# A two-layer relational graph convolution: edge tiles grouped by eight, one wait, one placing product and one addition per group

## The chip, the cores and the metric

The kernel runs on one core of one Trainium2 chip. The metric is the device time of one execution in microseconds (us); the number quoted is the median of three executions. A separate execution was recorded by the hardware profiler; it has its own time, which is given beside its span below.

## What is computed

The graph has N = 12,500 nodes with C = 128 float32 features and E = 200,000 edges, sorted by destination. The type of an edge (10 relations) is the argmax over ten of the 42 columns of its attributes. Two layers of the following form, a relu between them, and a layer norm over the sum with the input:

```python
seg  = dst * NUM_REL + edge_type
sums = segment_sum(x[src], seg, N * NUM_REL)
cnt  = segment_sum(ones, seg, N * NUM_REL)
mean = (sums / maximum(cnt, 1)[:, None]).reshape(N, NUM_REL, -1)
layer(x) = einsum('nrd,rdo->no', mean, w_rel) + x @ root + bias
...
h = relu(layer1(x))
out = layernorm(x + layer2(h))
```

So each layer reads 200,000 rows of 512 bytes by index, sums them by (destination, relation), divides by the count, multiplies each relation's means by that relation's 128x128 matrix and adds over relations.

## The kernel before

**Tiles.** The edges are cut into 1563 tiles of 128 (`NT`). Since they are sorted, the destinations of a tile lie in a window of at most 12 nodes (`WN`) from its first; a flag is set on the chip where that or another assumption fails, and a general program at the end of the file then does the work over (it is not run with these inputs).

**Per tile, in a layer** (`edges`). `gather` lets GpSimd (POOL) issue an indirect DMA that brings the 128 source rows to SBUF (L352). VectorE (DVE) makes a 128x120 matrix `oh` (L366): in an edge's row, the column 12 x type + (destination - window start) holds the edge's weight, one over its count; all else is 0. TensorE (PE) multiplies the gathered rows with it (L368): `zp` holds, for each feature, the mean's contributions to 120 (relation, node) pairs. In the profile a float32 matmul appears as two passes. ScalarE (ACT) copies four tiles at a time to `zs` (L369). For every 16 tiles ten products, one per relation with its 128x128 matrix as the stationary operand and 16x12 = 192 moving columns, accumulate `po` in PSUM (L373). Then, for each tile, DVE adds 12 columns of `po` to `acc`, a 128 x 12,628 array of features by nodes that stays in SBUF (L381); where, comes from a register loaded from the list of window starts `bt` (L376). The groups at the end have 8 and 3 tiles.

**Blocks.** When all edges of a block of 512 nodes are surely past (a fixed slack of 10 tiles), it is finished (25 blocks, the last of 212 nodes): the block's own rows are loaded and transposed (L297, copied by ACT in L299), the root product and the transposed sums are accumulated (L302, L303). In layer 1 (`hidden`) relu and the store to `hD` follow (L317), in layer 2 (`final`) the residual, the statistics, the normalisation and the store of the output (L332 to L342). `acc` is cleared behind each block.

**Preparation.** For each chunk of 128 tiles (13 chunks): `sources` loads source indices, casts them (L121), transposes them on PE (L113) and leaves the index list `idxE` (L114); `types` finds the relations (L180 to L185), keys and flags; `count` compares each edge's key with its 40 neighbours on either side, one shift at a time (L259, 40 compares and 80 products with the identity, L260 and L261, which add them up), and leaves the weights `wE`. Chunk 0 (and the sources and types of chunk 1) are prepared ahead of layer 1; the others in steps between the tiles of layer 1, by `between`, which takes as many steps as bring the chunk to its end eight tiles before it is needed.

**Order.** The instructions of each engine stand in the order of the program as scheduled; every tile buffer comes from a pool, and a new use waits for the last reader of the old one. `gpool` holds 22 buffers of four tiles, so POOL may run 88 tiles ahead of PE. `dpool` holds 12 one-hot matrices, `ps_z` three PSUM buffers of four tiles, `ps_o` a single one for `po`. Loads and stores of blocks and of preparation go through the queue of SyncE (SP). POOL waits for nothing but its index list, the buffers of the ring and, in layer 2, the store of `hD`. At the start DVE clears the whole of `acc` with one instruction (L155).

Of the kernel before, what the change touches and what calls it, by code (L numbers as in the profile page):

```python
# [9 lines left out]
F32 = mybir.dt.float32  # L10
BF16 = mybir.dt.bfloat16
I32 = mybir.dt.int32
# [14 lines left out]
Q = 4  # L27
G = 16
RING = 22
# [3 lines left out]
SLACK = 10  # L33
# [7 lines left out]
def rgcn_resnorm_kernel(ctx: ExitStack, tc: tile.TileContext, x, src, dst, attr, w_rel1, root1, b1,  # L41
# [12 lines left out]

    nc = tc.nc
# [5 lines left out]
    NCH = -(-NT // CT)  # L61
    NPAD = N + W
    NBLK = -(-N // YB)
# [15 lines left out]
    prep = fast.enter_context(tc.tile_pool(name="prep", bufs=2))  # L79
    msgp = fast.enter_context(tc.tile_pool(name="msgp", bufs=2))  # L80
    eqp = fast.enter_context(tc.tile_pool(name="eqp", bufs=6))
    gpool = fast.enter_context(tc.tile_pool(name="gpool", bufs=RING))
    dpool = fast.enter_context(tc.tile_pool(name="dpool", bufs=12))
    zpool = fast.enter_context(tc.tile_pool(name="zpool", bufs=2))
    ps_z = fast.enter_context(tc.tile_pool(name="ps_z", bufs=3, space=PSUM))
    ps_o = fast.enter_context(tc.tile_pool(name="ps_o", bufs=1, space=PSUM))
    ps_k = fast.enter_context(tc.tile_pool(name="ps_k", bufs=1, space=PSUM))
    ps_c = fast.enter_context(tc.tile_pool(name="ps_c", bufs=1, space=PSUM))
# [20 lines left out]
    def to_edges(to, t, c):  # L109

        p = chunk_rows(c)
        pt = ps_c.tile([P, P], F32, name="pt")
        nc.tensor.transpose(pt[:, :p], t[:p], ident[:p, :p])  # L113
        nc.vector.tensor_copy(to[:, c * CT:c * CT + p], pt[:, :p])  # L114
# [14 lines left out]

    thr_i = const.tile([P, NCH], I32, name="thr_i")  # L130
    nc.gpsimd.iota(thr_i, pattern=[[CT, NCH]], base=-SLACK, channel_multiplier=1)
    pads = const.tile([P, L + 1], I32, name="pads")
    nc.gpsimd.iota(pads, pattern=[[1, L + 1]], base=FAR, channel_multiplier=0)
    lane = const.tile([P, P], F32, name="lane")
# [8 lines left out]
    thr = const.tile([P, NCH], F32, name="thr")  # L143
    nc.vector.tensor_scalar(thr_i, thr_i, 6, None, op0=ALU.arith_shift_right)
    nc.vector.tensor_scalar(thr, thr_i, float(YB), None, op0=ALU.mult)
# [5 lines left out]
    nc.vector.tensor_tensor(own, own, lane, op=ALU.add)  # L151
    fl = const.tile([P, 1], F32, name="fl")
    nc.vector.memset(fl, 0.0)
    acc = const.tile([P, NPAD], F32, name="acc")
    nc.vector.memset(acc, 0.0)  # L155
# [5 lines left out]
    bt = keep.tile([1, NT], I32, name="bt")  # L161
# [25 lines left out]
    def types(c):  # L187
# [13 lines left out]
        nc.sync.dma_start(bt[:, c * CT:c * CT + n], bass.AP(dst.tensor, b, [[1, 1], [P, n]]))  # L201
        if last:
            nc.sync.dma_start(bt[:, NT - 1:NT], bass.AP(dst.tensor, dst.offset + E - P, [[1, 1], [1, 1]]))
# [392 lines left out]
```

## Time and profile before

| | |
|---|---|
| median of 3 runs | 4014.53 us (4013.73 to 4018.22) |
| the profiled execution's own time | 4817.36 us |
| its span, first to last instruction | 4815.5 us |
| mean granted TensorE clock in it | 0.706 |
| POOL busy, of it in gathers | 2971.9 us, 2970.6 us |
| PE busy | 2439.3 us |
| DVE busy | 1585.0 us |
| ACT busy | 470.9 us |
| longest single wait of POOL (for `hD`, between the layers) | 74.2 us |

The profiled execution is 803 us longer than the median of the others. The page gives, for each engine, the time in which it executed instructions; for groups of instructions (line, engine, output<-input, shape, count) the busy time, the mean length of one in ns, and the idle time of the engine just before them with what ended most of it. "issue" there is idle time that ended without anything waited for. In the waits, the three figures are the total in us, how often, and the longest. In the timeline, each row has its start in us, its length, engine, line and operation, and in brackets the idle time ahead of it and what ended it.

### The profile page before, as it was taken

To read this page: it belongs to the slowest core of one execution; us is meant where nothing else is said; L and a number is where in the kernel's file an instruction comes from. 1 tells how busy PE (TensorE), PEld (TensorE's weight loads), DVE (VectorE), ACT (ScalarE), POOL (GpSimd) and SP (SyncE) were. 2 spreads that over 40 slices of the span, in tenths; PEclk is the share of its full clock that TensorE was granted. 3 is DMA by queue.
4 is the path that set the end of the run, shared out by engine and by line. 5 is a ranking of instruction groups with operands and counts; after the bars stand their busy time and mean duration, and the time that the engine had idled before them with its cause. 6 is when DMAs were issued, how large, how long until landed. Compare 5 with 4: busy or idle time off the path is not lost.

```text
span 4815.5 us, 44360 instructions
## 1 busy us (share of the span) xinstructions
PE 2439.3 (51%) x12272; PEld 2184.5 (45%) x12272; DVE 1585.0 (33%) x7623; ACT 470.9 (10%) x899; POOL 2971.9 (62%) x3136
## 2 busy tenths in 40 slices
PE   0456655655655565665615444444444444444456
PEld 0445554545555455555514443444444444444445
DVE  3333443344334333333302222232222322232234
ACT  0001110111011111111100100000000000000001
POOL 6566666666666666666266666666666666666661
PEclk9766676676767676666756677777777776776777
DMA  5121222122122221112111221112111211121110
GB/s 163 41 75 51 79 76 75 53 76 75 51 80 74 56 55 52 50 51 54 32 48 46 55 53 49 49 52 55 50 51 51 57 51 50 50 56 49 51 52 25
DMA packets 180408, 279.04 MB, mean 58 GB/s; under 512 B 55448, under 2 KB 127015, under 8 KB 177031
## 3 DMA queue, kind: packets, MB, share of 16 engines
q0 software_dynamic: 100032, 205.07, 16.2%
q1 hardware_dynamic: 76957, 69.59, 4.6%
q8 instruction: 108, 1.77, 0.2%
q10 hardware_dynamic: 3168, 1.44, 0.1%
q14 instruction: 143, 1.17, 0.1%
HBM read 262.28 MB, written 13.60 MB: 57 GB/s over the span
## 4 chain that ended last, share of the span: by engine, by line
PE 29%; issue 27%; another core or an unknown queue 24%; DVE 8%; POOL 7%; ACT 2%; DMA 1%; DVEq 1%; SPq 0%; ACTq 0%; POOLq 0%
PE zp L368 14%; PE po L373 12%; POOL g L352 7%; DVE oh L366 4%; DVE acc L381 3%; ACT zs L369 1%; PE pf L303 1%; PE pt L261 1%; PE pt L260 1%; PE pf L302 1%; DMA g<-in_x_dram,idxE 1%; DVEq L376 1%; ACT fT L299 0%; PE pf L297 0%
## 5 line engine op out<-in xcount | busy, mean ns | idle before, releaser
L352 POOL DMA_INDIRECT g<-hD,idxE x1563 | 1477.4, 945 | 946.9 <-issue 429.4
L368 PE MATMUL zp<-oh,g 128*128 128x120 f32 x6252 | 1269.8, 364 | 1551.8 <-issue 1001.8
L352 POOL DMA_INDIRECT g<-in_x_dram,idxE x1563 | 1493.2, 955 | 802.9 <-issue 416.1
L368 PEld LDWEIGHTS zp<-oh,g 128*128 128x128 f32 x6252 | 1134.9, 267 | 1675.4 <-issue 1105.0
L366 DVE TENSOR_SCALAR oh<-iota,keyE,wE 128x120 f32<-128x120 f32 x3126 | 1028.5, 351 | 675.4 <-remote 340.8
L381 DVE TENSOR_TENSOR acc<-acc,po 128x12 f32 x3126 | 518.1, 166 | 2032.6 <-remote 1268.1
L373 PE MATMUL po<-zs,w 128*128 128x192 f32 x3960 | 916.7, 386 | 439.6 <-issue 225.3
L373 PEld LDWEIGHTS po<-zs,w 128*128 128x128 f32 x3960 | 807.2, 232 | 507.5 <-issue 301.7
L369 ACT ACTIVATE zs<-zp 128x480 f32<-128x480 f32 (+1 forms) x782 | 417.8, 570 | 3650.1 <-remote 2408.5
L259 DVE TENSOR_TENSOR eqb<-kp,kh 128x129 bf16<-128x129 f32 (+43 forms) x520 | 148.4, 305 | 196.5 <-remote 145.3
L260 PE MATMUL pt<-eqb,identb 128*128 128x128 bf16 (+1 forms) x520 | 120.9, 269 | 160.0 <-issue 130.7
L261 PE MATMUL pt<-eqb,identb 128*128 128x128 bf16 (+1 forms) x520 | 121.6, 275 | 52.6 <-issue 49.7
L261 PEld LDWEIGHTS <-identb 128*128 128x128 bf16 (+1 forms) x520 | 62.8, 121 | 176.2 <-issue 170.3
L302 PE MATMUL pf<-root,fT 128*128 128x128 f32 x392 | 105.3, 359 | 55.9 <-issue 41.0
L303 PE MATMUL pf<-ident,a 128*128 128x128 f32 x392 | 107.4, 365 | 13.9 <-issue 8.1
L302 PEld LDWEIGHTS pf<-root,fT 128*128 128x128 f32 x392 | 84.3, 263 | 63.9 <-issue 48.0
L260 PEld LDWEIGHTS <-identb 128*128 128x128 bf16 (+1 forms) x520 | 66.8, 129 | 75.4 <-issue 74.9
L303 PEld LDWEIGHTS pf<-ident,a 128*128 128x128 f32 x392 | 88.2, 270 | 22.5 <-issue 14.5
L299 ACT ACTIVATE fT<-pf 128x512 f32<-128x512 f32 (+1 forms) x50 | 29.3, 587 | 498.7 <-remote 245.3
L332 DVE TENSOR_TENSOR v<-pf,xb 128x512 f32<-128x512 f32 (+2 forms) x26 | 17.1, 660 | 174.7 <-remote 127.3
L297 PE MATMUL pf<-ident,hb 128*128 128x128 f32 x98 | 21.9, 356 | 23.9 <-DVE v L332 17.6
L342 DVE TENSOR_SCALAR o<-v,mv,rstd 128x128 f32<-128x128 f32 x98 | 27.8, 349 | 0.2
(71 smaller groups left out, 371.6 us busy)
## 6 DMA issues: line engine op xcount, KB each, us to landing
m<-in_edge_attr_dram SPq DMA_DIRECT2D x24, 1344.0 KB
g<-in_x_dram,idxE POOLq DMA_INDIRECT x1563
g<-hD,idxE POOLq DMA_INDIRECT x1563
xb<-in_x_dram SPq DMA_DIRECT2D x48, 256.0 KB
hD<-hb SPq DMA_DIRECT2D x24, 256.0 KB
hb<-hD SPq DMA_DIRECT2D x24, 256.0 KB
out_dram<-o SPq DMA_DIRECT2D x24, 256.0 KB
w<-in_L_gnn_w_rel_dram ACTq DMA_DIRECT2D x2, 640.0 KB
```

Of the source, the lines that this page charges most:

```text
L259: nc.vector.tensor_tensor(eq[:p, :P + d], kp[:p, L - d:L + P], kh[:p, L:L + P + d], op=ALU.is_equal)
L260: nc.tensor.matmul(pc[:p], identb[:p, :p], eq[:p, :P], start=(d == 1), stop=False)
L261: nc.tensor.matmul(pc[:p], identb[:p, :p], eq[:p, d:d + P], start=False, stop=(d == L))
L302: nc.tensor.matmul(pr[:h, t, :], fT[:, t * P:t * P + h], rsb[l], start=True, stop=False)
L303: nc.tensor.matmul(pr[:h, t, :], a[:, t * P:t * P + h], ident, start=False, stop=True)
L352: nc.gpsimd.indirect_dma_start(out=g[:, j, :], out_offset=None, in_=table, in_offset=bass.IndirectOffsetOnAxis(ap=idxE[:, t0 + j:t0 + j + ...
L366: nc.vector.tensor_scalar(oh, iota[:, :KW], keyE[:, t:t + 1], wE[:, t:t + 1], op0=ALU.is_equal, op1=ALU.mult)
L368: nc.tensor.matmul(zp[:, j, :], g[:, j, :], oh, start=True, stop=True)
L369: nc.scalar.activation(zs[:, :, q:q + m, :], zp[:, :m].rearrange("c j (r n) -> c r j n", n=WN), AF.Copy)
L373: nc.tensor.matmul(po[:, :n], wsb[l][:, r, :], zs[:, r, :n], start=(r == 0), stop=(r == NREL - 1))
L376: _, offs = nc.values_load_multi_w_load_instructions(bt[0:1, t0 + j0:t0 + j0 + m], engines=[DVE], min_val=0, max_val=N - 1, skip_runtime_b ...
L381: nc.vector.tensor_tensor(acc[:, s], acc[:, s], po[:, j0 + j], op=ALU.add)
```

## The change

- A group is 8 tiles, in both layers. One-hot matrices, gathered rows and `zp` have one buffer per group; the ring is 13 groups, 104 tiles. Of the eight zp products of a group the last tile's is issued first, and it alone waits, for all eight gathers.
- The projection takes the sums as the stationary operand (up to 96 columns, node slots of 8 tiles) and the relation's matrix as 128 moving columns. Its result has node slots on partitions; ACT copies it to SBUF (`ms`). A second product multiplies it with a 96x80 matrix `at` of zeros and ones that DVE makes for each group; it places the slots of all 8 tiles in a window of 80 nodes (`pa`), with features on partitions again. One DVE addition of 128x80 per group takes it into `acc`; four groups' positions are loaded into registers at a time.
- The stages of three groups are interleaved: sums of one, then placing and addition of an older, then projection of the one between.
- `types` makes the slots' positions (`place`) with a small product per chunk and a check of their width; 25 loads of single destinations serve a check that a block was not finished too early. The time at which a block is finished comes from a formula (`done_after`); blocks are 24 of 512 nodes, then 128 and 84.
- `count` compares 8 shifts in one instruction (5 instead of 40) and adds them with 20 products of 512 columns instead of 80 of 128; a reduction adds the four parts.
- The preparation's pools have one buffer instead of two.
- `acc` is cleared at the start in pieces of 512 columns, written ahead of `sources(1)`; it isn't cleared behind the blocks of layer 2. The flag's reduction stands between the layers instead of behind the second.

The constants for the slots' positions, the small loads into `b8_i` and the lines in which only names of PSUM tiles change are left out of the diff below.

```diff
-Q = 4
-G = 16
-RING = 22
+G = 8
+QB = 4
+SW = 80
+RING = 13
+DB = 8
 L = 40
 CT = 128
 YB = 512
-SLACK = 10
...
-    NBLK = -(-N // YB)
+    starts = list(range(0, N - YB // 2, YB))
+    starts += list(range(starts[-1] + YB, N, P)) if N - starts[-1] > YB else []
+    NBLK = len(starts)
+    def done_after(k):
+        if k == NBLK - 1:
+            return NT
+        f = starts[k + 1] / N
+        return min(NT, int((E * f + 5 * (E * f * (1 - f)) ** 0.5) / P) + 2)
...
-    prep = fast.enter_context(tc.tile_pool(name="prep", bufs=2))
-    msgp = fast.enter_context(tc.tile_pool(name="msgp", bufs=2))
-    eqp = fast.enter_context(tc.tile_pool(name="eqp", bufs=6))
+    prep = fast.enter_context(tc.tile_pool(name="prep", bufs=1))
+    eqp = fast.enter_context(tc.tile_pool(name="eqp", bufs=2))
     gpool = fast.enter_context(tc.tile_pool(name="gpool", bufs=RING))
-    dpool = fast.enter_context(tc.tile_pool(name="dpool", bufs=12))
-    zpool = fast.enter_context(tc.tile_pool(name="zpool", bufs=2))
-    ps_z = fast.enter_context(tc.tile_pool(name="ps_z", bufs=3, space=PSUM))
+    dpool = fast.enter_context(tc.tile_pool(name="dpool", bufs=3))
+    zpool = fast.enter_context(tc.tile_pool(name="zpool", bufs=3))
+    spool = fast.enter_context(tc.tile_pool(name="spool", bufs=3))
+    ps_z = fast.enter_context(tc.tile_pool(name="ps_z", bufs=2, space=PSUM))
     ps_o = fast.enter_context(tc.tile_pool(name="ps_o", bufs=1, space=PSUM))
-    ps_k = fast.enter_context(tc.tile_pool(name="ps_k", bufs=1, space=PSUM))
-    ps_c = fast.enter_context(tc.tile_pool(name="ps_c", bufs=1, space=PSUM))
+    ps_a = fast.enter_context(tc.tile_pool(name="ps_a", bufs=1, space=PSUM))
...
     acc = const.tile([P, NPAD], F32, name="acc")
-    nc.vector.memset(acc, 0.0)
...
-    bt = keep.tile([1, NT], I32, name="bt")
+    bt = keep.tile([1, NG], I32, name="bt")
+    place = keep.tile([GR, NCH * CT // G], F32, name="place")
+    wide = const.tile([P, 1], F32, name="wide")
+    nc.vector.memset(wide, 0.0)
+    late_i = const.tile([1, NBLK], I32, name="late_i")
 
...
-        nc.sync.dma_start(bt[:, c * CT:c * CT + n], bass.AP(dst.tensor, b, [[1, 1], [P, n]]))
-        if last:
-            nc.sync.dma_start(bt[:, NT - 1:NT], bass.AP(dst.tensor, dst.offset + E - P, [[1, 1], [1, 1]]))
+        ng = -(-p // G)
+        nc.sync.dma_start(bt[:, c * CT // G:c * CT // G + ng], bass.AP(dst.tensor, b, [[1, 1], [G * P, ng]]))
+        b8_i = prep.tile([G, CT // G], I32, name="b8_i")
...
+        for k in range(NBLK):
+            t = done_after(k)
+            if c * CT <= t < c * CT + p:
+                nc.sync.dma_start(late_i[:, k:k + 1], bass.AP(dst.tensor, dst.offset + t * P, [[1, 1], [1, 1]]))
...
-        nc.vector.tensor_scalar(bt[:, c * CT:c * CT + p], bt[:, c * CT:c * CT + p], 0, N - 1, op0=ALU.max,
-                                op1=ALU.min)
+        g0 = c * CT // G
+        nc.vector.tensor_scalar(bt[:, g0:g0 + ng], bt[:, g0:g0 + ng], 0, N - 1, op0=ALU.max, op1=ALU.min)
+        b8 = prep.tile([G, CT // G], F32, name="b8")
+        nc.vector.tensor_copy(b8[:, :ng], b8_i[:, :ng])
+        pw = ps_f.tile([P, YB], F32, name="pf")
+        nc.tensor.matmul(pw[:GR, :ng], rank, b8[:, :ng], start=True, stop=True)
+        nc.vector.tensor_scalar(place[:, g0:g0 + ng], pw[:GR, :ng], within, None, op0=ALU.add)
+        reach = prep.tile([GR, 1], F32, name="reach")
+        nc.vector.tensor_reduce(reach, place[:, g0:g0 + ng], axis=AX.X, op=ALU.max)
+        nc.vector.tensor_tensor(wide[:GR], wide[:GR], reach, op=ALU.max)
...
-        kp = ps_k.tile([P, P + 2 * L], F32, name="kp")
-        nc.scalar.activation(kp[:p], kh[:p], AF.Copy)
-        pc = ps_c.tile([P, P], F32, name="pt")
-        for d in range(1, L + 1):
-            eq = eqp.tile([P, P + L], BF16, name="eqb")
-            nc.vector.tensor_tensor(eq[:p, :P + d], kp[:p, L - d:L + P], kh[:p, L:L + P + d], op=ALU.is_equal)
-            nc.tensor.matmul(pc[:p], identb[:p, :p], eq[:p, :P], start=(d == 1), stop=False)
-            nc.tensor.matmul(pc[:p], identb[:p, :p], eq[:p, d:d + P], start=False, stop=(d == L))
-            if d % 2 == 0:
-                yield
+        kp = ps_f.tile([P, YB], F32, name="pf")
+        nc.scalar.activation(kp[:p, :P + 2 * L], kh[:p], AF.Copy)
+        pc = ps_f.tile([P, 4, P], F32, name="pf")
+        R = P + L
+        for d in range(1, L + 1, DB):
+            eq = eqp.tile([P, DB, R], BF16, name="eqb")
+            ahead = bass.AP(kh.tensor, kh.offset + d, [[kh.ap[0][0], p], [1, DB], [1, R]])
+            nc.vector.tensor_tensor(eq[:p], kp[:p, None, :R].to_broadcast([p, DB, R]), ahead, op=ALU.is_equal)
+            for k in range(0, DB, 4):
+                nc.tensor.matmul(pc[:p], identb[:p, :p], eq[:p, k:k + 4, L:], start=(d + k == 1), stop=False)
+                back = bass.AP(eq.tensor, eq.offset + k * R + L - d - k, [[eq.ap[0][0], p], [R - 1, 4], [1, P]])
+                nc.tensor.matmul(pc[:p], identb[:p, :p], back, start=False, stop=(d + k + 3 == L))
+            yield
         wp = prep.tile([P, P], F32, name="wp")
-        nc.vector.tensor_scalar(wp[:p], pc[:p], 1.0, None, op0=ALU.add)
+        nc.vector.tensor_reduce(wp[:p], pc[:p].rearrange("p k e -> p e k"), axis=AX.X, op=ALU.add)
+        nc.vector.tensor_scalar(wp[:p], wp[:p], 1.0, None, op0=ALU.add)
...
-        nc.vector.memset(acc[:, n0:n0 + n], 0.0)
+        if l == 0:
+            nc.vector.memset(acc[:, n0:n0 + n], 0.0)
...
-        g = gpool.tile([P, Q, C], F32, name="g")
+        g = gpool.tile([P, G, C], F32, name="g")
+        return g, [nc.gpsimd.indirect_dma_start(out=g[:, j, :], out_offset=None, in_=table, in_offset=(
+            bass.IndirectOffsetOnAxis(ap=idxE[:, t0 + j:t0 + j + 1], axis=0))) for j in range(n)]
+    whole = mybir.DependencyInfo(mybir.DependencyClass.Sync, mybir.DependencyReason.DATA)
+    def sums(table, t0, n):
+        g, gathers = gather(table, t0, n)
+        oh = dpool.tile([P, G, KW], F32, name="oh")
         for j in range(n):
...
+            t = t0 + j
+            nc.vector.tensor_scalar(oh[:, j, :], iota[:, :KW], keyE[:, t:t + 1], wE[:, t:t + 1], op0=ALU.is_equal,
+                                    op1=ALU.mult)
+        at = spool.tile([GR, SW], F32, name="at")
+        nc.vector.tensor_scalar(at, iota[:GR, :SW], place[:, t0 // G:t0 // G + 1], None, op0=ALU.is_equal)
+        zp = ps_z.tile([P, G // QB, YB], F32, name="zp")
+        for j in reversed(range(n)):
+            m = nc.tensor.matmul(zp[:, j // QB, j % QB * KW:(j % QB + 1) * KW], g[:, j, :], oh[:, j, :],
+                                 start=True, stop=True)
+            if j < n - 1:
+                tc.keep_in_program_order(m)
+                continue
+            for d in gathers[:j]:
+                tc.add_manual_dep(m.ins, d.ins.name, whole, reason="one wait per group")
+        return zp, at
+    def project(l, n, zp):
 
         zs = zpool.tile([P, NREL, G, WN], F32, name="zs")
...
+        for b in range(-(-n // QB)):
+            m = min(QB, n - b * QB)
+            nc.scalar.activation(zs[:, :, b * QB:b * QB + m, :],
+                                 zp[:, b, :m * KW].rearrange("c (j r n) -> c r j n", r=NREL, n=WN), AF.Copy)
+        po = ps_o.tile([P, C], F32, name="po")
         for r in range(NREL):
-            nc.tensor.matmul(po[:, :n], wsb[l][:, r, :], zs[:, r, :n], start=(r == 0), stop=(r == NREL - 1))
...
+            nc.tensor.matmul(po[:n * WN], zs[:, r, :n].rearrange("c j n -> c (j n)"), wsb[l][:, r, :],
+                             start=(r == 0), stop=(r == NREL - 1))
+        ms = spool.tile([GR, C], F32, name="ms")
+        nc.scalar.activation(ms[:n * WN], po[:n * WN], AF.Copy)
+        return ms
+    offs = []
+    def add(t0, n, ms, at):
+        pa = ps_a.tile([P, SW], F32, name="pa")
+        nc.tensor.matmul(pa, ms[:n * WN], at[:n * WN], start=True, stop=True)
+        if not offs:
+            g0 = t0 // G
+            offs.extend(nc.values_load_multi_w_load_instructions(
+                bt[0:1, g0:min(NG, g0 + 4)], engines=[DVE], min_val=0, max_val=N - 1,
+                skip_runtime_bounds_check_because=HELD)[1])
+        s = ds(offs.pop(0), SW)
+        nc.vector.tensor_tensor(acc[:, s], acc[:, s], pa, op=ALU.add)
 
     def layer(table, l, finish, steps):
 
         done = 0
...
+        held, projected = [], []
+        def project_oldest():
+            t0, n, zp, at = held.pop(0)
+            projected.append((t0, n, project(l, n, zp), at))
+        def add_oldest():
+            nonlocal done
+            t0, n, ms, at = projected.pop(0)
+            add(t0, n, ms, at)
+            while done < NBLK and t0 + n >= done_after(done):
                 finish(done)
                 done += 1
+        for t0 in range(0, NT, G):
+            n = min(G, NT - t0)
+            held.append((t0, n, *sums(table, t0, n)))
+            if projected:
+                add_oldest()
+            if len(held) > 1:
+                project_oldest()
+            if steps:
+                till, left, s = steps[0]
+                for _ in range(max(1, -(-left[0] // max(1, till - t0 // G)))):
+                    left[0] -= 1
+                    if next(s, steps) is steps:
+                        steps.pop(0)
+                        break
+        while held or projected:
+            if projected:
+                add_oldest()
+            if held:
+                project_oldest()
 
...
+    for a in range(0, NPAD, YB):
+        nc.vector.memset(acc[:, a:min(NPAD, a + YB)], 0.0)
     sources(1)
     for _ in chain(types(0), types(1)):
...
-        todo.append((c * CT - 8, [8 + L // 2 + 2], chain(*s, count(c))))
+        todo.append((c * CT // G - 2, [8 + L // DB + 2], chain(*s, count(c))))
     layer(x, 0, hidden, todo)
-    layer(hD, 1, final, [])
+    late = const.tile([1, NBLK], F32, name="late")
+    for k in range(NBLK):
+        if done_after(k) < NT:
+            nc.vector.tensor_scalar(late[:, k:k + 1], late_i[:, k:k + 1], float(starts[k + 1]) - 0.5, None, op0=ALU.is_lt)
+        else:
+            nc.vector.memset(late[:, k:k + 1], 0.0)
+    nc.vector.tensor_scalar(wide, wide, float(SW) - 0.5, None, op0=ALU.is_gt)
+    nc.vector.tensor_tensor(fl, fl, wide, op=ALU.max)
     pf = ps_f.tile([P, YB], F32, name="pf")
     nc.tensor.transpose(pf[0:1, :P], fl, ident)
-    flag_f = const.tile([1, 1], F32, name="flag_f")
-    nc.vector.tensor_reduce(flag_f, pf[0:1, :P], axis=AX.X, op=ALU.max)
-    nc.vector.tensor_copy(flag_i, flag_f)
+    flag_f = const.tile([1, 2], F32, name="flag_f")
+    nc.vector.tensor_reduce(flag_f[:, 0:1], pf[0:1, :P], axis=AX.X, op=ALU.max)
+    nc.vector.tensor_reduce(flag_f[:, 1:2], late, axis=AX.X, op=ALU.max)
+    nc.vector.tensor_tensor(flag_i, flag_f[:, 0:1], flag_f[:, 1:2], op=ALU.max)
+    layer(hD, 1, final, [])
     fast.close()
```

## The prediction

> **What bounds the kernel now.** I read the page's table of busy shares first, then the groups and the waits, and last the timeline of single stretches. The median to explain is 4014.53 us. The profiled execution took 4817.36 us, span 4815.5 and 1.9 outside it, so it is 803 us longer than the median; a prediction needs to know which part of it is in the plain runs too.
>
> ```profile
> PE 2439.3 (51%) x12272; PEld 2184.5 (45%) x12272; DVE 1585.0 (33%) x7623; ACT 470.9 (10%) x899; POOL 2971.9 (62%) x3136
> ...
> L352 POOL DMA_INDIRECT g<-hD,idxE x1563 | 1477.4, 945 | 946.9 <-issue 429.4
> L352 POOL DMA_INDIRECT g<-in_x_dram,idxE x1563 | 1493.2, 955 | 802.9 <-issue 416.1
> ```
>
> No engine is full; POOL is busiest, all of it in gathers (L352), one per tile and layer. Its waits, and its timeline at the end of a layer:
>
> ```profile
> POOL g L352 <- issue: 845.5, 2763, 1.8
> POOL g L352 <- PE zp L368: 479.2, 124, 6.1
> POOL g L352 <- remote: 196.4, 101, 14.7
> ```
>
> ```profile
> 2297.02 0.94 POOL L352 DMA_INDIRECT g<-in_x_dram,idxE  x1 [0.30 <-issue]
> 2372.20 0.94 POOL L352 DMA_INDIRECT g<-hD,idxE  x1 [74.24 <-DMA hD<-hb]
> ```
>
> "Issue" is 845.5/2763 = 0.306 us ahead of nearly every gather, waiting for nothing. A gather of 0.94 us and its gap repeat every 1.2487 us ((3182.16-3163.43)/15, in a stretch without waits). That is the number everything rests on: 1563 gathers make 1562 x 1.2487 = 1950.5 us a layer. Layer 1's total is 1493.2-1563x0.944 = 17 us more, layer 2's 1.6. Now the plain run as this stream plus its ends: first gather at 15.39; 1967.5; from the last gather of layer 1 to layer 2's first 31.1 (2.74 until PE may read it, as from 2372.20 to the first zp at 2374.94, and 28.4 from the last three tiles' zp at 2343.83 to 2372.20); 1952.1; tail 2.74 and 46.2 (last zp's end, about 4769.3, to 4815.5); 1.9 outside. Sum 4016.9, within 0.1% of the median. So the plain runs have no room for POOL's waits for the ring (479.2, 196.4 and smaller ones): they, and a layer gap of 74 instead of 30, are the profiled execution's 803 us. The kernel is a gather stream with three ends.
>
> Whether PE keeps pace is read where POOL is silent. The rows of the two stretches after a layer's last gather:
>
> ```profile
> 4724.51 3.83 PE L368 MATMUL zp<-oh,g 128*128 128x120 f32 x32 [1.81 <-ACT zs L369]
> 4729.63 3.52 PE L373 MATMUL po<-zs,w 128*128 128x192 f32 x20 [1.29 <-DVE acc L381]
> 4733.86 3.83 PE L368 MATMUL zp<-oh,g 128*128 128x120 f32 x32 [0.72 <-ACT zs L369]
> ```
>
> Sixteen tiles pass in 9.35 us (4724.51 to 4733.86), 0.58 us each against 1.25 of the gather. Beside gathers the same trace has PE taking a pass in 2 to 3 us with "issue" ahead of it (2429 to 2456 us): stalls that end with the gathers, and that the sum has no place for.
>
> **What the Trainium skill says.** "DMA: Bandwidth & Descriptors", section on the anatomy of a gpsimd-issued DMA, gives about 2.0 us of fixed cost, mostly completion: the trace has 2.74 from the gather's start to PE, of which 0.94 is POOL's; they pipeline, so the 1.25 stands. "Perfetto Trace Analysis", on such instructions, says that GpSimd's processors write the descriptors in place of a hardware block: 0.94 us for every gather, whichever table it reads, agrees. "SBUF — State Buffer", on who interferes, says that a DVE instruction with two SBUF inputs contends with a GpSimd one that reads SBUF: gathers of 1.2 to 1.5 us in layer 1 lie beside argmax's L182 and L183, which fits the 17 us. "TensorE: Matmul & The Clock Gate", on what is happening, says that PE runs at half clock after idling: passes here take 0.12 us (3.83/32) or 0.21 to 0.22 (the tail's 36-column po: 4.45/20), so I cost PE at both.
>
> **The change, part by part.**
>
> *Gathers.* 3126 as before, one a tile, same rows. Removed 0, added 0: the stream stays 1967.5 + 1952.1. POOL's few more iotas at the start are of 0.1 to 0.3 us each, before its first gather and beside DVE's clearing; nothing.
>
> *PE's load.* Per 8 tiles: 16 zp passes, 20 po passes (ten float32 products, now for 8 tiles instead of 16), 2 placing passes: 38, against 26. At 0.12 us 4.6 us, at 0.22 8.4 us, in the 9.99 us that 8 gathers take (8x1.2487). Finish adds 12 matmuls (24 passes) every 64 tiles, layer 1 the counts besides (20 matmuls of 512 columns instead of 80 of 128, every 128 tiles). Hidden under the gathers while a pass stays below about (9.99-0.9)/38 = 0.239 us; above that it is the rival below.
>
> *One wait per 8 tiles.* The first zp pass waits for the last of eight gathers; the other fifteen, the po of the group before and everything behind them on PE wait with it. This delays PE by up to seven gathers, 8.7 us, but nobody waits for it except the ring, which grows from 88 to 104 tiles (110 to 130 us of gathers). Cost 0, at the two layer ends counted below.
>
> *Additions and register loads.* 3126 additions of 0.166 us, with register loads between them, become 392 of 128x80, each between 0.166 (128x12) and 0.35 (L342, 128x128). No gain: DVE, at 33% of the span, is hidden under the gathers, and the one-hots (3126, 1028.5 us) stay. ACT gets one copy of 128 columns more a group, under the 0.57 of its 480-column copy (L369), in 9.99: hidden.
>
> *Counting by 8 shifts, single prep buffers.* 40 compares of 0.305 become 5 of 128x1344; hidden while the 104-tile ring holds. SP has about 61 transfers ahead of the first keys' load in place of 24; SP's rows for such small loads are 0.4 to 0.9 us each, so at 0.6 the first counts start 22 us later than the 49 us of the trace. The ring is full only at 9.7+104x1.2487 = 139 us, which leaves some 68 for the counts. Cost 0; if that cover went, each us late is a us.
>
> *Clearing in pieces.* Before:
>
> ```profile
> 3.52 10.58 DVE L155 MEMSET acc<- 128x12628 f32 x1 [2.60 <-issue]
> 14.02 0.16 DVE L121 CAST s_f<-s_i 128x128 f32<-128x128 int32 x1
> ...
> 15.39 1.11 POOL L352 DMA_INDIRECT g<-in_x_dram,idxE  x1 [13.50 <-DVE own L151]
> ```
>
> The first index list (L121) stands behind the whole clear. In the changed program's order on DVE, 4 pieces stand ahead of that cast and 8 more between it and the index copy. The 13 pieces of 512 columns, at 10.58x512/12628 = 0.43 us: 12 make 5.2, so 3.5+5.2+1.4 (cast to gather, 15.39-14.02) = 10.1; if the source rows' arrival rules, 8.5. I take 9.7: gain 5.7, bounds 3 to 9.
>
> *Between the layers.* Before, behind the last zp: one po of 16 tiles (3.48), an addition chain of 4.43, po of 8 and 3 with the last waits, root, relu, store: 28.4 us. After: the last group of 3 needs zp, copy, po (20 passes), copy, placing (2), addition, then a block of only 84 nodes instead of 212. In the changed order, PE has behind the last zp two po (40 passes), three placing products (6) and the last three blocks' finish (36 passes at most). Estimate: 82 passes are 10 us at 0.12 or 18 at 0.22; the copies, additions, relu and the store between them come to 7 to 10.5. So 17 to 28.5; I take 23: gain 5.4, bounds 0 to 12.
>
> *Tail.* Before, behind the last zp:
>
> ```profile
> 4771.03 3.52 PE L373 MATMUL po<-zs,w 128*128 128x192 f32 x20 [0.87 <-DVE acc L381]
> 4778.99 6.51 PE L373 MATMUL po<-zs,w 128*128 128x192 f32 x20 [4.43 <-DVE acc L381]
> ...
> 4799.78 4.45 PE L373 MATMUL po<-zs,w 128*128 128x36 f32 x20 [2.73 <-DVE acc L381]
> ```
>
> po has one buffer, so each next one waits for 16 separate additions (4.43). That goes; the flag's matmul and reductions move between the layers' programs, where they stand beside the first gathers. What comes late next is the layernorm of the last blocks: 84 rows' worth of v, statistics, o and a store, some 10 us as before. With the sum above plus this, 22 to 33.5; I take 29: gain 17, bounds 5 to 24 (and not below 0, since every removed wait was on the path).
>
> *Sum.* 9.7 + 1967.5 + 2.74+23 + 1952.1 + 2.74+29 + 1.9 = 3988.7, 28 less than the same sum before; taken from the median, 4014.5-28 = 3986.5. Predicted 3987.
>
> **Rivals.**
>
> *A, the forecast:* the stream binds, the ends get shorter. Its own range from the bounds: gains of 8 to 44, 3971 to 4006. For it: the closing sum. Chance 0.66.
>
> *B, the ends give nothing:* three stages of 8 tiles at slow passes, with the last group's extra copy and placing, make gap and tail as long as before, and only the start's few us remain: 4007 to 4022, within 0.2% (8 us, about what this measurement can tell from no change). For it: PE idles between groups, so slow passes at the end are likely. Chance 0.13.
>
> *C, slower: PE becomes the bound.* Place: po, now twice as often, 38 passes a group. If PE idles while it waits for eight gathers and starts each burst slow, passes cost 0.22 and more with gaps at each change of tile; it decides from 0.239 us a pass. At 0.26: 38x0.26+0.9 = 10.8 against 9.99, 8% on 3920: about 4320. For it: 0.22 is common in the trace, and layer 1 has finish and counts as well. Against: a PE that is busy throughout has fast passes. Chance 0.12.
>
> *D, the stalls of the profiled execution are real:* the plain interval would be shorter than 1.25 (the median less stalls), and fewer instructions and waits would take several per cent: 3600 to 3950. Against: it needs an interval that no row shows. Chance 0.09.
>
> **How the numbers follow.** Faster: A nearly whole, and D: 0.75. Same: B: 0.13. Slower: C: 0.12. The range 3965 to 4014 is A's bounds, a little beyond on the short side for the estimated passes, and half of B; what lies outside is C, D and the rest of B.
>
> **What would show it.** Gathers still 1.2487 us apart with 0.94 each; first gather near 10 us; the stretch from layer 1's last gather to layer 2's first near 26; last gather to the end near 32; PE and DVE idle ahead of each group on gathers. POOL waiting on zp for whole stretches while PE has no gap speaks for C. An interval below 1.2 us would show the premise wrong, and the sum with it.

## The result, and the profile after

| | before | changed |
|---|---|---|
| median | 4014.43 us (20 runs, 4012.07 to 4020.32) | 4021.74 us (20 runs, 4016.72 to 4028.73) |
| ratio | 1 | 1.0018, 95% interval 1.0012 to 1.0025 |

So the change costs 7 us where 28 were to be gained. The changed kernel's profiled execution took 4026.78 us, close to its median, and its trace has none of the long stalls in which the one before stood. The waits of POOL and its groups on the page, changed kernel:

```profile
POOL g L404 <- issue: 929.2, 3049, 0.3
POOL g L404 <- DMA hD<-hb: 19.5, 1, 19.5
```

```profile
L404 POOL DMA_INDIRECT g<-in_x_dram,idxE x1563 | 1521.9, 974 | 482.4 <-issue 464.5
L404 POOL DMA_INDIRECT g<-hD,idxE x1563 | 1498.9, 959 | 495.5 <-issue 464.7
```

Inside a layer POOL stands only in the fixed 0.3 us ahead of each gather: the stream of gathers does set the pace. But a gather takes 974 and 959 ns on the mean, not the 955 and 945 of before. The ends of the two layers in POOL's timeline:

```profile
9.28 1.29 POOL L404 DMA_INDIRECT g<-in_x_dram,idxE  x1 [6.33 <-DVE lane L172]
...
2006.27 0.94 POOL L404 DMA_INDIRECT g<-in_x_dram,idxE  x1 [0.30 <-issue]
2026.74 0.94 POOL L404 DMA_INDIRECT g<-hD,idxE  x1 [19.53 <-DMA hD<-hb]
...
4000.67 0.94 POOL L404 DMA_INDIRECT g<-hD,idxE  x1 [0.30 <-issue]
```

The kernel before is compared through a run of it whose only edit is the clearing in pieces (e4 below), since that profiled execution is undisturbed too (span 4009.5). Its same four gathers:

```profile
8.71 1.51 POOL L351 DMA_INDIRECT g<-in_x_dram,idxE  x1 [6.83 <-DVE lane L150]
...
1976.54 0.95 POOL L351 DMA_INDIRECT g<-in_x_dram,idxE  x1 [0.30 <-issue]
2008.21 0.94 POOL L351 DMA_INDIRECT g<-hD,idxE  x1 [30.72 <-DMA hD<-hb]
...
3962.50 0.94 POOL L351 DMA_INDIRECT g<-hD,idxE  x1 [0.30 <-issue]
```

Subtracting starts gives the whole account (start of before: 15.39 of its own trace):

| us | before | changed | difference | predicted |
|---|---|---|---|---|
| first gather | 15.4 | 9.3 | -6.1 | -5.7 |
| stream, layer 1 | 1967.8 | 1997.0 | +29.2 | 0 |
| between the layers | 31.7 | 20.5 | -11.2 | -5.4 |
| stream, layer 2 | 1954.3 | 1973.9 | +19.6 | 0 |
| last gather to the end | 47.0 | 24.4 | -22.6 | -17 |
| sum | | | +8.9 | -28 |

The ends give 40 us; the stream takes 49 back. The +8.9 compares two single traces, the medians differ by 7.3. Below, a stream's length is last start less first start of a layer; without any stretch it is 1562 x 1.2487 = 1950.5.

### The profile page after: what moved, and what is told of

Its sections match the earlier page's. It is cut to its first block, busy times and chain, and to the rows that moved or that the text cites. A ratio compares the mean times of both kernels' runs of the same rounds, so it can differ in the third digit from the quotient of the medians.

```text
span 4025.1 us, 45940 instructions
## 1 busy us (share of the span) xinstructions
PE 2499.6 (62%) x16184; PEld 2382.6 (59%) x16184; DVE 1345.0 (33%) x4911; ACT 566.0 (14%) x1293; POOL 3023.0 (75%) x3142
## 4 chain that ended last, share of the span: by engine, by line
POOL 61%; issue 28%; PE 6%; DMA 5%; DVE 0%; ACT 0%; POOLq 0%; ACTq 0%
POOL g L404 61%; DMA g<-in_x_dram,idxE 2%; PE zp L421 2%; DMA g<-hD,idxE 2%; PE po L440 2%; PE pf L355 1%; PE pf L356 1%; PE pf L350 0%; PE pa L451 0%; DVE acc L506 0%; DMA s_i<-in_src_dram 0%; DMA hD<-hb 0%; ACT ms L443 0%; POOLq L404 0%; DVE acc L458 0%
## 5 line engine op out<-in xcount | busy, mean ns | idle before, releaser
L415 DVE TENSOR_SCALAR oh<-iota,keyE,wE 128x120 f32<-128x120 f32 x3126 | 858.6, 346 | 1905.3 <-PE zp L421 1905.2
L440 PE MATMUL po<-w,zs 128*96 128x128 f32 x7840 | 1068.8, 297 | 0.6 <-ACT zs L436 0.6
L440 PEld LDWEIGHTS po<-w,zs 128*96 128x96 f32 x7840 | 1018.7, 185 | 1.5 <-ACT zs L436 0.9
L443 ACT ACTIVATE ms<-po 96x128 f32<-96x128 f32 x392 | 106.9, 273 | 703.5 <-PE po L440 703.2
L451 PE MATMUL pa<-at,ms 96*128 96x80 f32 (+1 forms) x784 | 184.2, 329 | 1.6 <-ACT ms L443 1.4
L451 PEld LDWEIGHTS pa<-at,ms 96*128 96x128 f32 (+1 forms) x784 | 172.9, 271 | 2.8 <-ACT ms L443 2.8
L418 DVE TENSOR_SCALAR at<-iota,place 96x80 f32<-96x80 f32 x392 | 107.1, 273 | 0.0
L309 DVE TENSOR_TENSOR eqb<-pf,kh 128x1344 bf16<-128x1344 f32 (+1 forms) x65 | 100.2, 1549 | 14.5 <-PE pf L313 13.9
L311 PE MATMUL pf<-eqb,identb 128*128 128x512 bf16 (+1 forms) x130 | 50.0, 384 | 16.4 <-DVE eqb L309 16.4
L313 PE MATMUL pf<-eqb,identb 128*128 128x512 bf16 (+1 forms) x130 | 50.2, 386 | 0.0
L352 ACT ACTIVATE fT<-pf 128x512 f32<-128x512 f32 (+2 forms) x52 | 29.9, 575 | 11.3 <-PE pf L350 6.6
L313 PEld LDWEIGHTS <-identb 128*128 128x128 bf16 (+1 forms) x130 | 12.7, 97 | 26.6 <-issue 18.4
```

The source lines that it names most:

```text
L309: nc.vector.tensor_tensor(eq[:p], kp[:p, None, :R].to_broadcast([p, DB, R]), ahead, op=ALU.is_equal)
L415: nc.vector.tensor_scalar(oh[:, j, :], iota[:, :KW], keyE[:, t:t + 1], wE[:, t:t + 1], op0=ALU.is_equal, op1=ALU.mult)
L418: nc.vector.tensor_scalar(at, iota[:GR, :SW], place[:, t0 // G:t0 // G + 1], None, op0=ALU.is_equal)
L440: nc.tensor.matmul(po[:n * WN], zs[:, r, :n].rearrange("c j n -> c (j n)"), wsb[l][:, r, :], start=(r == 0), stop=(r == NREL - 1))
L443: nc.scalar.activation(ms[:n * WN], po[:n * WN], AF.Copy)
L451: nc.tensor.matmul(pa, ms[:n * WN], at[:n * WN], start=True, stop=True)
```

## What stretches the gathers: first four runs

In the changed kernel's trace the longer gathers lie beside VectorE's one-hots:

```profile
3195.35 0.27 DVE L418 TENSOR_SCALAR at<-iota,place 96x80 f32<-96x80 f32 x1
3195.55 1.84 DVE L415 TENSOR_SCALAR oh<-iota,keyE,wE 128x120 f32<-128x120 f32 x7
3196.64 1.42 POOL L404 DMA_INDIRECT g<-hD,idxE  x1 [0.30 <-issue]
```

Seven one-hots stand back to back from 3195.55 to 3197.39; the gather begun in them takes 1.42 us instead of 0.94. Of 273 gathers of layer 2 that begin in a run of seven or more (up to 0.2 us before its end), 212 take longer than 0.96 us; the mean over all 273 is 0.072 us above the undisturbed 0.944. This mean excess is what is compared below as the stretch of "a gather begun in a run".

**e1, one-hots made once.**

```diff
-            nc.vector.tensor_scalar(oh[:, j, :], iota[:, :KW], keyE[:, t:t + 1], ...)
+    # ahead of the layers, for j in range(G)
+    nc.vector.tensor_scalar(oh[:, j, :], iota[:, :KW], float(j), 0.25, ...)
```

> The changed kernel with the eight one-hot matrices made once, ahead of the layers, and used by every group (so the sums are taken with fixed columns and weights and the result is not the reference's; all else runs). Theory 1: the stream of gathers got longer because VectorE now makes eight one-hots in one run, and a gather beside that run is stretched; in the trace of the changed kernel gathers are 76.6 us longer in sum than at 0.94 us each, some 45 of it beside one-hots. Without them 4021.7 - 45 = about 3977, layer 2's gathers nearly all 0.94. Theory 2: the stretch comes from something else that changed (preparation, the additions of 80 columns, waits for eight gathers): 4010 to 4022.

Measured 3973.58 us; streams 1967.4 and 1951.5. Theory 1 holds so far: layer 2 is within 1 us of unstretched.

**e2, the counting row read from PSUM.** All one-hots are made, in runs of eight.

```diff
+    pb = ps_a.tile([P, YB], F32, name="pb")
+    iota_p = pb[:, P:P + KW]
+    nc.vector.tensor_copy(iota_p, iota[:, :KW])
...
-            nc.vector.tensor_scalar(oh[:, j, :], iota[:, :KW], ...)
+            nc.vector.tensor_scalar(oh[:, j, :], iota_p, ...)
...
-        pa = ps_a.tile([P, SW], F32, name="pa")
+        pa = pb[:, :SW]
```

> The changed kernel; the one-hots are made as before, in runs of eight, but VectorE reads the counting row from PSUM instead of SBUF. Theory 1a: VectorE holds the ports that it shares with GpSimd only while both input and output are in SBUF; then the stretch goes and about 3980 is measured, though each one-hot may be slower. Theory 1b: a run of one-hots stretches the gather wherever it reads: 4018 to 4025. Theory 2 as well: no change.

Measured 3969.96, ratio to before 0.9892 (0.9877 to 0.9907); streams 1968.4 and 1951.0. One run in its timeline, and gathers begun in it:

```profile
3246.57 0.94 POOL L404 DMA_INDIRECT g<-hD,idxE  x1 [0.30 <-issue]
3247.82 0.95 POOL L404 DMA_INDIRECT g<-hD,idxE  x1 [0.31 <-issue]
```

```profile
3246.29 0.24 DVE L461 TENSOR_TENSOR acc<-acc,pb 128x80 f32 x1 [2.15 <-PE pb L454]
3246.45 2.57 DVE L415 TENSOR_SCALAR oh<-pb,keyE,wE 128x120 f32<-128x120 f32 x8
```

The run is longer, with one-hots 0.311 us apart against 0.252 from SBUF (medians in the runs of layer 2), and harms nobody: of 334 gathers begun in a run one is longer than 0.96. It too follows another instruction without a pause, here the addition, which ends at 3246.53. This is what the Trainium skill leads to expect, "VectorE: DVE Perf Modes", section on mode 2×_2P: a single-source instruction takes both read ports only with source and destination in SBUF, since PSUM has one read port; and "SBUF — State Buffer", on who interferes, says that in that mode VectorE contends with GpSimd, and that the first to start has the ports for its whole instruction. The trace agrees on when they contend; on how long, see the end.

**e3, each one-hot behind its own gather.**

```diff
-            nc.vector.tensor_scalar(oh[:, j, :], ...)
+            h = nc.vector.tensor_scalar(oh[:, j, :], ...)
+            tc.add_manual_dep(h.ins, gathers[j].ins.name, whole, reason="one-hot after its gather")
```

> The changed kernel; each one-hot waits for the gather of its own tile, so eight are made over ten us instead of in one run of two. Theory 1 says that it's the run: gathers fall back to nearly 0.94 in layer 2 and about 3980 to 3990 is measured. If each one-hot costs its share wherever it lies, no change: 4018 to 4025.

Measured 3979.09; streams 1963.5 and 1951.4. One-hots from SBUF, spread in this way, do no harm. The 9 us more than e2 lie at the ends: 24.9 us between the layers and 29.9 behind the last gather, against 15.6 and 23.4.

**e4, the kernel before with the clearing in pieces** (the memset loop of the changed kernel, in place of L155).

> The kernel before with the clearing at the start cut into pieces of 512 columns, as in the changed kernel. By the sum of the prediction the first gather moves from 15.4 to about 9.3 us and all behind it with it: 4014.4 - 6 = 4008.4. If something else rules the start, 4014.

Measured 4009.21, ratio 0.9984 (0.9977 to 0.9990): -5.9, as reckoned.

## Each part by itself: four runs

**e5, the kernel before with the counting row in PSUM** (in the bank of `kp`; L366 reads it there).

> The kernel before, with its single one-hots reading the counting row from PSUM. In the undisturbed trace of the kernel before (with the clearing in pieces) layer 2's gathers are only 6.5 us longer in sum than at 0.94 each, 3 of it beside one-hots. If it is the runs of eight that made the changed kernel's stream long, there is little to win here: 4014.5 - 5 = 4009, between 4005 and 4014. If single one-hots stretch gathers too, it would gain as the changed kernel did, some 45: 3970.

Measured 3995.39, a miss: the forecast was 4005 to 4014. The gain is not from the gathers: its streams are 1964.4 and 1953.9, together some 4 us shorter than e4's. In its trace the time between the layers is 20.0 instead of 31.7, because the scheduler now puts the projection of the last group of 16 ahead of the last sums. What follows these, in e4 and then in e5:

```profile
1978.88 1.18 PE L367 MATMUL zp<-oh,g 128*128 128x120 f32 x4 [1.39 <-DMA g<-in_x_dram,idxE]
1979.85 5.22 PE L372 MATMUL po<-zs,w 128*128 128x192 f32 x20
```

```profile
1982.41 1.01 PE L371 MATMUL zp<-oh,g 128*128 128x120 f32 x4 [1.41 <-DMA g<-in_x_dram,idxE]
1983.21 2.30 PE L376 MATMUL po<-zs,w 128*128 128x96 f32 x10
```

In e5 the projection of 192 columns (16 tiles) is gone from there. Of the rest, 8 us lie between its profiled execution (4003.36, the slowest of five) and the median; they stay unexplained.

**e6, the search for the relation with second operands in PSUM too** (on top of e2).

```diff
-        top = pool.tile([P, n], F32, name="top")
+        top = pool.tile([P, n], F32, name="top") if n == 1 else top_p
+        ri = riota if n == 1 else riota_p
...
-        nc.vector.tensor_tensor(eq[:p], eq[:p], riota[:p, None, :]. ...
+        nc.vector.tensor_tensor(eq[:p], eq[:p], ri[:p, None, :]. ...
```

> The changed kernel with the counting row in PSUM, and in the search for the relation the maximum and the row of ranks, the second operands of its two comparing instructions, in PSUM too. The prediction put 17 us of layer 1's gathers down to these two instructions with two SBUF inputs. If so, layer 1's sum falls from 20.6 us over 0.94 to some 7 and the time from 3970 to about 3957. If the stretch there has another cause, 3970.

Measured 3955.36, ratio 0.9856 (0.9840 to 0.9871). Its groups on the page:

```profile
L411 POOL DMA_INDIRECT g<-hD,idxE x1563 | 1475.8, 944 | 491.9 <-issue 459.9
L411 POOL DMA_INDIRECT g<-in_x_dram,idxE x1563 | 1478.2, 946 | 481.7 <-issue 459.3
```

Layer 1 falls to 946 ns a gather, its stream to 1953.2. So the two instructions with two SBUF inputs did cost 15 us here (in the kernel before, which has the same two, it was not tried). This version beats both kernels.

**e7, the kernel before with runs of eight.**

```diff
+            if q % 8 == 0:
+                oh = dpool.tile([P, 8, KW], F32, name="oh")
+                for j in range(min(8, n - q)):
+                    t = t0 + q + j
+                    h = nc.vector.tensor_scalar(oh[:, j, :], iota[:, :KW], keyE[:, t:t + 1], ...)
+                    if len(added) > 16:
+                        tc.add_manual_dep(h.ins, added[-17].ins.name, behind, reason="one run of eight")
```

> The kernel before with this one part alone: its one-hots are made eight at a time in one run (three buffers of eight instead of twelve of one, 76 tiles in the ring instead of 88 to make room). Theory 1: each run stretches a gather by 0.10 to 0.15 us, 196 times a layer, so 4014.4 + 40 to 50 = about 4058. Theory 2, that the stretch needs the rest of the change: 4014 to 4018.

A miss: 3993.41. The ends moved with the order (between the layers 19.6, tail 27.2), which alone is -32; but the streams, 1970.7 and 1957.9, grew by 6 us, not by 40. Yet the runs are there, two of them often joined:

```profile
3442.68 3.87 DVE L367 TENSOR_SCALAR oh<-iota,keyE,wE 128x120 f32<-128x120 f32 x15
3443.36 0.98 POOL L352 DMA_INDIRECT g<-hD,idxE  x1 [0.30 <-issue]
3444.65 0.95 POOL L352 DMA_INDIRECT g<-hD,idxE  x1 [0.30 <-issue]
```

The mean stretch is 0.02 us for 218 gathers begun in a run, against 0.07. So in these kernels a run from SBUF is needed (e2, e3), but is not enough. Theory 1 as it stood falls.

**e8, own waits instead of one for eight** (e2 with the reversed order and the added waits of `sums` taken out).

> The changed kernel with the counting row in PSUM; each of a group's eight products waits for its own gather, in order, instead of one wait for all eight. By the prediction that wait costs nothing and saves nothing while the gathers set the pace: 3970, within 3. If sharing the wait shortens PE's work enough to matter at the ends, longer by some us; if its delay of up to seven gathers is paid at the layer's ends, shorter by 1 to 3.

Measured 3967.49, within the 3 us forecast, and the ratio's interval (0.9867 to 0.9898) overlaps e2's. The shared wait costs nothing once the gathers aren't stretched.

## What a run needs to do harm: six runs

**e9 and e11, the runs moved.** Each one-hot also waits: in e9 for the last product of a projection, in e11 for the last copy to `zs` (`pos` collects these instructions; `pos[-3]` and `pos[-2]` are those of the group that lets the run start).

```diff
+            if len(pos) > 2:
+                tc.add_manual_dep(h.ins, pos[-3].ins.name, whole, reason="behind the projection")
```

> The changed kernel, counting row in SBUF; the run of eight one-hots of a group waits besides for the end of a projection (the one that TensorE does right behind the sums whose end lets the run start now), so that VectorE's run no longer lies beside TensorE's 20 passes and ScalarE's two copies. Open after the run of eights in the kernel before, which hardly stretched the gathers: in layer 2 of the changed kernel 45 of 50 gathers beside a run are hit by 0.08 us on the mean, there 92 of 246 by 0.02. Theory 1c: it takes the run together with the other engines' work: gathers of layer 2 fall from 26.8 us over 0.94 to about 8 and the time from 4021.7 to about 3990. Theory 1d: the run does it wherever it lies, and the difference comes from where the buffers lie in SBUF or from chance of phase: 4015 to 4025.

> The changed kernel, counting row in SBUF; the run of eight one-hots waits for ScalarE's two copies of the sums whose end lets it start now, some 1.0 us after that end, but not for TensorE's projection, which lasts some 2.8 us from there. If ScalarE's copies are what makes a run stretch a gather, layer 2 falls to about 8 us over 0.94, as behind the projection, and the time to about 3993. If it is TensorE's row of passes, more than half of the run still lies beside them: 4008 to 4018.

e9: 3995.62, streams 1982.7 and 1955.6. e11: 3983.06, streams 1980.7 and 1958.7 (of a profiled execution of 3993.83, 11 us above its median). Both are mild in layer 2, 0.010 and 0.015 us a gather begun in a run. e9 seemed to prove that it takes the other engines' work; e11 denies it for TensorE, whose projection lies beside most of that run. And the gather of 1.42 us above starts at 3196.64, when ScalarE's copies (in the same trace until 3195.73) are over. Theory 1c falls.

**e10, other addresses** (the pools `gpool` and `dpool` change places).

> The changed kernel with the pool of the one-hot matrices taken ahead of the ring of gathered rows, so that both lie at other addresses in SBUF; nothing else changes. If the place of the buffers decides how far a run stretches a gather, the time moves by 10 us or more, down to 3985; if not, 4018 to 4025.

Measured 4022.06; streams 1995.1 and 1973.7. So moving the buffers changes nothing.

The three mild kinds of run (e7, e9, e11) begin with an instruction that waits, and only after the instruction ahead has ended (in e7 0.04 us after, the median of layer 2). The harmful seven follow the placing matrix without such a pause: they start 0.08 us before it ends, on the median of layer 2.

**e13, e15, e16: one wait at the head of the run.** e13 puts all eight directly behind the addition and the placing matrix, by order alone. e15 and e16 keep that order and make the one-hots wait for VectorE's own addition, or its own placing matrix; in the traces only the first of a run carries the wait. Shown is e13's edit; e15 has the other arguments, and in e16 `pos` collects the placing matrices.

```diff
+    # e13: NoSync, SCHED_ONLY; e15 and e16: Sync, DATA
+    after_it = mybir.DependencyInfo(...)
...
+            if len(pos) > 2:
+                tc.add_manual_dep(h.ins, pos[-3].ins.name, after_it, reason="behind the addition")
```

> The changed kernel, counting row in SBUF; only VectorE's order is changed: all eight one-hots directly behind the addition and the placing matrix, in place of one ahead of these and seven behind. No wait is added. If a pause ahead of the run (as in the runs behind the projection and behind the copies) is what lets the gathers through, they stay stretched, 0.07 us on the mean, and 4015 to 4025 is measured. If it was the split, or the mere shift, 3985 to 3997.

> The kernel with the eight one-hots directly behind the addition and the placing matrix (4023.8 us), and the run's first one-hot now waits for the end of that addition, which has mostly passed by then. If a waiting instruction at the head of the run is what matters, about 3992; if only a real pause does, between; if it is the moment at which the run lies beside the other engines, 4018 to 4026.

> The same, the run's first one-hot waiting for the end of the placing matrix directly ahead of it: a pause of about 0.1 us between them. If a pause ahead of the run lets the gathers through, about 3992 and 0.01 to 0.02 us a gather begun in a run; if it is the moment at which the run lies, 4018 to 4026 and 0.07.

| | median us | stream 1 | stream 2 | stretch of a gather begun in a run, us (layer 2) |
|---|---|---|---|---|
| e13, no wait | 4023.80 | 1995.0 | 1973.3 | 0.069 |
| e15, wait for the addition | 4001.51 | 1983.9 | 1964.3 | 0.041 |
| e16, wait for the placing matrix | 3996.50 | 1987.8 | 1955.8 | 0.012 |

One place each in the timelines of e13 and then e16:

```profile
3229.88 0.25 DVE L420 TENSOR_SCALAR at<-iota,place 96x80 f32<-96x80 f32 x1
3230.05 2.10 DVE L415 TENSOR_SCALAR oh<-iota,keyE,wE 128x120 f32<-128x120 f32 x8
...
3230.20 1.10 POOL L404 DMA_INDIRECT g<-hD,idxE  x1 [0.30 <-issue]
```

```profile
3244.16 0.25 DVE L420 TENSOR_SCALAR at<-iota,place 96x80 f32<-96x80 f32 x1
3244.44 2.35 DVE L415 TENSOR_SCALAR oh<-iota,keyE,wE 128x120 f32<-128x120 f32 x8
...
3245.76 0.98 POOL L404 DMA_INDIRECT g<-hD,idxE  x1 [0.30 <-issue]
```

In e13 the run starts 0.17 us after the placing matrix, while that still drains; in e16 0.28 after, once it is done. The run then is longer (2.35 against 2.10) and the gather shorter: with the pause it is more often VectorE that gives way. In layer 2, 251 one-hots of e16 take longer than 0.43 us, against 128 of e13; the usual length is 0.33. A tenth of a microsecond of pause per group brings layer 2 from 1973.3 to 1955.8. Chance of phase, the rival left by theory 1d, is not the reason: of gathers that begin 0.50 to 0.75 us into a run there are 41 in each trace, stretched by 0.145 us in e13 and 0.015 in e16. In layer 1 the pause helps only by 7 us of 27; that VectorE's preparation there fills such pauses is likely, but was not tried.

The pause is not all of it either. In e15 the first one-hot starts 0.17 us after the placing matrix on the median, just as in e13, and only carries a wait that has mostly passed; yet the stretch falls from 0.069 to 0.041. Why a passed wait helps is not shown.

**e14, the shared wait undone with the row in SBUF** (as e8, without e2).

> The changed kernel with this one part undone: each product waits for its own gather, in order, instead of one wait for eight. The runs of one-hots stay as they are. If the runs are the cause and the shared wait costs nothing, 4019 (the 2.5 us of the run with the counting row in PSUM less), within 4. If the stretch comes from the shared wait, 3975 to 3985.

Measured 4010.26, a miss of both forecasts; streams 1991.0 and 1967.8, and 0.057 us a gather begun in a run. The runs stay harmful, so the shared wait isn't their main cause. But it makes them worse: undoing it gains 11 us, 6 in each stream, and the ratio's interval (0.9980 to 0.9997) lies clear of the changed kernel's. How it does so stays open.

**e12, e6 with own waits.**

> The changed kernel with the counting row and the operands of the search for the relation in PSUM (3955 us), and each product waiting for its own gather (2.5 us less in the run with the counting row in PSUM alone): the two add up to about 3953. 3903 is 3126 gathers at 1.2487 us, so no more than some 50 us of start, layer change and tail are left.

Measured 3956.03, the same as e6 within the intervals, where 3953 was expected. Streams 1954.5 and 1951.1: nearly all that is left above POOL's own time is the ends.

## Why the prediction was wrong

- *The gather stream sets the time, and the stalls of the profiled execution are not in plain runs:* right. Without the stalls, e4's trace closes at 4009.5 with the parts of the prediction's sum: 31.7 between the layers (31.1 there), 47.0 behind the last gather (48.9), streams of 1967.8 and 1954.3 (1967.5 and 1952.1).
- *"Removed 0, added 0: the stream stays 1967.5 + 1952.1":* the step that failed, by +49. The working counted POOL's instructions and took 17 us of contention over unchanged, but asked of VectorE only whether it had time to spare. Its one-hots, 3126 as before, came to stand in runs of eight, seven of them behind another instruction without a pause, and these hold the gathers up: with the one-hots made once the streams lose 52.0 us (e1), with their source in PSUM 51.5 (e2). That VectorE is hidden at 33% of the span was true of its own time and wrong as a conclusion. The prediction used what the skill says of two SBUF inputs and left aside what the same section says of single-source instructions in a two-port mode, which the one-hots are by e2's outcome.
- *17 us of layer 1 put down to two instructions with two SBUF inputs:* too much for the trace that it was read from. There 8.5 us of the excess lies in gathers beside them and 6.4 us in 55 gathers beside one-hots, so gathers longer beside one-hots could be seen before the change. In the changed kernel the two cost 15 us (e6).
- *Clearing in pieces:* -5.7 reckoned, -6.1 in the trace, -5.9 by itself (e4).
- *One wait per 8 tiles, "Cost 0":* right where the one-hots don't stretch the gathers (e8, e12), wrong for the changed kernel as it stood: there the wait is 12 us of the 49 (e14). The ring does hide PE's delay; that the wait also bears on the stretch was not foreseen.
- *Between the layers and tail:* the mechanism was right, both gains within their bounds and above the value taken: 11.2 for 5.4 and 22.6 for 17. The prediction costed passes midway between 0.12 and 0.22. Behind the last sums of the changed kernel they run at the fast end:

```profile
4008.74 2.36 PE L440 MATMUL po<-w,zs 128*96 128x128 f32 x20
```

  20 passes in 2.36 are 0.12 us each. Before, one of the two projections of 16 that stood in that place, in e4:

```profile
3975.99 5.60 PE L372 MATMUL po<-zs,w 128*128 128x192 f32 x20 [4.74 <-DVE acc L380]
```

- *Rival B, "the ends give nothing":* the time landed in its band (4007 to 4022) by chance: the ends gave 40, and the stream took 49. *Rival C, TensorE as the bound:* not seen; inside a layer POOL stands for nothing longer than its fixed 0.3 us. *Rival D:* refuted, no interval is shorter.
- *Single preparation buffers, 8 shifts at once:* no cost seen; with the row in PSUM layer 1's stream is 1968.4, as in e4 (1967.8).

## What to carry to other kernels

When GpSimd's descriptor-writing stream sets the pace, VectorE's instructions are part of its cost even where VectorE is mostly idle: look at which of them read and write SBUF alone, and at how they stand together, not at their sum. Giving such an instruction one operand in PSUM took its conflict away, although each became slower (e2, 52 us less). Spreading the one-hots gave 43 of that (e3), a short pause ahead of a row of them 25 (e16). When a change batches work, ask of each engine that loses its pauses who used them.

## What was not expected of the hardware

- The stretch depends on what stands ahead of the run: with the same instructions in the same order, 0.069 us a gather begun in a run without a pause and 0.012 with one of about 0.1 us (e13, e16). A gather held up by 0.48 us has waited longer than one one-hot takes (0.33 us, with starts 0.25 apart), and one instruction is what the section cited at e2 speaks of; so several in a row seem able to hold one gather up. How the turn is given was not found out.
- In a row, one-hots of 128x120 start 0.311 us apart with their source in PSUM, 0.252 from SBUF.
- 3126 gathers at 1.2487 us are 3903 us; the best version, 3955, is 1.3% above.
